# Transforms along w as 64x64 quarter products, and a second spectral layer worked in groups of 192 channels

## The chip, the core and the metric

The kernel runs on one core of one Trainium2 chip, as a single program. The metric is the device time in microseconds of one execution; the time before is the median of three runs. A profile was taken of one further execution. The engines are PE (TensorE, matrix products; its weight loads are shown apart as PEld), DVE (VectorE), ACT (ScalarE), POOL (GpSimd) and SP (SyncE, which here only issues DMAs). All data are float32, and one float32 product of the program appears in the trace as two matmul records, one for each pass.

## What is computed

The input x is one image of 48 x 48 positions with 768 channels. Four layers follow each other: an attention block with an MLP, a spectral layer (L1), a diffusion scan along channels with an output projection (L2), and a second spectral layer (L3) with weights of its own. The change concerns the two spectral layers and the places that feed them. One of them is, cut to what matters:

```python
xs = jnp.fft.rfft2(x, axes=(1, 2))              # 48 x 25 modes, 768 channels
xs = xs.reshape(B, H, Wm, NUM_HEADS, BLOCK)     # 8 blocks of 96 channels
o1r = relu(xr @ w1[0] - xi @ w1[1] + b1[0])     # per block, 96 -> 96
o1i = relu(xi @ w1[0] + xr @ w1[1] + b1[1])
o2r = o1r @ w2[0] - o1i @ w2[1] + b2[0]
o2i = o1i @ w2[0] + o1r @ w2[1] + b2[1]
out = irfft2(softshrink(o2r) + 1j * softshrink(o2i), s=(H, W))
return out + x
```

## The kernel before

Every Fourier transform is a product with a constant matrix. A spectral layer has three parts, and its data pass between them through two scratch tensors in HBM, `yu[0]` and `yu[1]`, one for each half of the channels (384 columns, `TB`).

The forward transform along w (`spectrum_rows`) takes the image in groups of eight image rows, held as four pairs of rows: 96 partitions (two rows of 48 positions) by 384 channels each. There are 12 such groups in a layer, six for each half. A group is four products with the block matrix `fw` (96 in, 112 out, L1495), four copies out of PSUM that alternate between ACT and DVE (`Evac`, L63 and L65), and one DMA to `yu` (L1497). In the first layer eleven of the groups are worked inside the MLP of the layer before, through `follow`, between the MLP's products, and the twelfth inside the spectral mix; in the second layer all twelve are worked inside the output projection of the scan (`so`, L1364), which leaves its result in SBUF as `x3`.

The mix (`spectrum_mix`) works through 40 items: 2 halves, 5 pieces of 5 frequencies (`kc`), 4 blocks of 96 channels. The items are pipelined by hand over five steps: in step n the kernel issues, in this order, the way back along h of item n-4 (`u`, L1609), the second layer of item n-3 (`z`, L1594 and L1595, then `cl` and `Z` on DVE), the first layer of item n-1 (`o`, L1573 to L1575), and the transform along h of item n (`x`, L1559). The pieces are loaded as `yt` (L1524), and the results `us` go back to `yu` (L1618), one DMA for each piece. In the first layer `yt` is added to `us` on DVE, so that the residual passes through the way back; in the second layer `us` is only copied, on ACT and DVE in turn. After each step a function `beside(step)` places other work.

The way back along w loads a group of eight rows as `gt` and multiplies it with `iw`: in the first layer by 24 products whose outputs have 96 columns (L1696), in the second by four full products (L1792), whose results DVE adds to `x3` (L1794), followed by a store to the output on ACT's queue. In the second layer the groups of half 0 go into the steps from 32 on; those of half 1 follow after the last item, with `gt` loaded in two parts, the four first pieces early and the rest after the last `us` has landed. The last group stores each pair of rows by itself.

The tile framework places semaphores by itself and may reorder instructions of one engine within its dependencies. All DMAs named here except the stores are issued by SP in the order that it is given; a DMA that waits holds those behind it.

Of the kernel before, what the change touches and what calls it, by code (L numbers as in the profile page):

```python
# [12 lines left out]
F32 = mybir.dt.float32  # L13
F32R = mybir.dt.float32r
AF = mybir.ActivationFunctionType
ALU = mybir.AluOpType
# [29 lines left out]
YR = 112  # L46
# [75 lines left out]


# [762 lines left out]
def mlp_phase(tc, ident, w1s_d, b1, w2, w2s_d, b2, ln_g, ln_b, xr_d, xa_d, follow_in):  # L886
# [8 lines left out]
    with (  # L895
# [14 lines left out]

        def psum(name):
            return pt.tile([P, 512], F32, tag="t", name=name)
# [180 lines left out]
def scan_phase(tc, ident, w, wts, rows_back, xh, x_close, c_d, cr_d, out_open):  # L1093
# [18 lines left out]
    K = 112  # L1112
# [5 lines left out]
    with tc.tile_pool(name="sc_s", bufs=1, side="left") as sp:  # L1118
# [3 lines left out]
        def out_weights():  # L1122
            wp = out_open("so_w")
            wo = wp.tile([P, 2, C], F32, tag="wo", name="wo")
            nc.sync.dma_start(wo, wo_d)
            return wo, load_bcast(nc, wp, bo_d, C, "bo", parts=BS)
# [203 lines left out]
        x3 = out_open("x3").tile([BS, NPR, C], F32, tag="x3", name="x3")  # L1330
        hg = s[ITERS % 2].rearrange("p n r t -> p (n r t)").rearrange("p (t n) -> p t n", t=NPR)
        with (
# [11 lines left out]
            def turned(j, q4):  # L1344
# [4 lines left out]
                hTs[j, q4] = tp.tile([P, 4, 2, G], F32, tag=f"hT{j}_{q4}", name=f"hT_{j}_{q4}", bufs=1)  # L1349
                nc.scalar.copy(hTs[j, q4], ps.rearrange("p (i s w) -> p i s w", i=4, s=2)[:, :, :, :G])  # L1350
# [4 lines left out]
            for half in range(2):  # L1355
                cols = slice(half * TB, (half + 1) * TB)
                for p2 in range(NPR // 2):
                    if half == 0 and p2 % 2 == 0:
                        turned(1, p2 // 2)
                    for t in range(2):  # L1360
                        pr = 2 * p2 + t
                        ps = psum(f"{pr}_{half}")
                        for j in range(2):
                            nc.tensor.matmul(ps[:BS, :TB], lhsT=hTs[j, pr // 4][:, pr % 4].rearrange("p s w -> p (s w)"), rhs=wo[:, j, cols], start=j == 0, stop=j == 1)  # L1364
                        t_ = tp.tile([BS, TB], F32, tag="t", name=f"st_{pr}_{half}")
                        V.tensor_tensor(t_, ps[:BS, :TB], bo[:, cols], ALU.add)
                        nc.scalar.activation(x3[:, pr, cols], t_, AF.Silu)
# [16 lines left out]
def block_kernel(ctx: ExitStack, tc: tile.TileContext, a: dict):  # L1384
# [69 lines left out]
    yu = [dram.tile([YR, G // 2, TB], F32, tag=f"yu{i}", name=f"yu{i}") for i in range(2)]  # L1454
    todo = []
    follow_in = lambda *args: afno_follow(nc, xa_d, a["fw2"], yu, todo, *args)
# [29 lines left out]

def spectrum_rows(nc, fw, x, yu, half, g, psum, pool, ev, name, bufs=2):

    ys = pool.tile([YR, 4, TB], F32, tag="ys", name=f"{name}_ys_{half}_{g}", bufs=bufs)
    for i in range(4):
        ps = psum(f"f_{half}_{g}_{i}")
        nc.tensor.matmul(ps[:YR, :TB], lhsT=fw, rhs=x[:, i, :], start=True, stop=True)  # L1495
        ev(ys[:, i, :], ps[:YR, :TB])
    nc.sync.dma_start(yu[half][:, 4 * g : 4 * g + 4, :], ys)  # L1497


def spectrum_open(tc, stack, name, a, layer, yu, side):  # L1500
# [3 lines left out]
    cp, yp = (stack.enter_context(tc.tile_pool(name=f"{name}_{n}", bufs=bufs, side=side)) for n, bufs in (("c", 1), ("y", 3)))  # L1504
# [16 lines left out]
    def load(half, kc):  # L1521
        if (half, kc) not in yts:
            yts[half, kc] = yp.tile([BS, KC, TB], F32, tag="yt", name=f"{name}_yt_{half}_{kc}")
            nc.sync.dma_start(yts[half, kc], yu[half][4 * KC * kc : 4 * KC * (kc + 1)].rearrange("(k q) p c -> (q p) k c", q=4))  # L1524
        return yts[half, kc]
# [4 lines left out]
def spectrum_mix(tc, name, opened, yu, psum, keep, side, halves, beside):  # L1530
# [7 lines left out]
    ev = Evac(nc)  # L1538
    HB = NB // 2
    (fh, w1t, w1s, w1d, w2t, b1t, ih), load = opened  # L1540
    with tc.tile_pool(name=f"{name}_s", bufs=2, side=side) as sp:
# [10 lines left out]
        def s_fft_h(i):  # L1552
            half, kc, b = items[i]
            if b == 0:
                ys[half, kc] = load(half, kc), sp.tile([BS, KC, TB], F32, tag="us", name=f"{name}_us_{half}_{kc}")
            yt = ys[half, kc][0]
# [9 lines left out]
        def s_mlp1(i):  # L1566
            half, kc, b = items[i]
            b += half * HB
# [18 lines left out]
        def s_mlp2(i):  # L1587
            half, kc, b = items[i]
            b += half * HB
# [13 lines left out]
        def s_ifft_h(i):  # L1603
            half, kc, b = items[i]
            Z = flow.pop(i)
            yt, us = ys[half, kc]
# [4 lines left out]
            if keep:  # L1611
                nc.vector.tensor_tensor(us[:, :, cols], pv, yt[:, :, cols], ALU.add)
# [317 lines left out]
```

## Time and profile before

| what | value |
|---|---|
| median of three runs | 3623.33 us (3620.8 to 3623.38) |
| profiled execution | 3626.7 us, span 3624.9 us, mean clock 0.987 |
| PE busy | 3539.1 us, 98% |
| DVE, ACT, POOL busy | 2002.9, 1138.5, 685.8 us |
| attention block up to its MLP | 0 to 1621 us |
| MLP, with 11 forward groups of L1 | 1621 to 2638 us |
| spectral layer L1, mix and half of its way back | 2638 to 2849 us |
| scan L2 | 2849 to 3290 us |
| output projection, with 12 forward groups of L3 | 3290 to 3386 us |
| mix of L3, with six ways back | 3386 to 3593 us |
| last reload, six ways back, stores | 3593 to 3625 us |

A row of a group of instructions gives the line, the engine, the operation, the tiles (written <- read), the shape, the count and the times; for matmuls the two numbers joined by a star are rows and columns of the array that the product uses. The record of a matmul contains its way through the array, so records of products that follow each other overlap, and the time that one takes is read from the distance between starts or from the chain of waits. The clock is the share of TensorE's full speed that was granted.

### The profile page before, as it was taken

Reading aid. Unit: us, or ns where it says so; the run is one execution under the profiler, and the core shown is the slowest. Engines: PE = TensorE matmul, PEld = TensorE weight load, DVE = VectorE, ACT = ScalarE, POOL = GpSimd, SP = SyncE. Lnnn points to the kernel's source line nnn. Section 1 sums busy time; section 2 is a strip of 40 time slices with the busy share of each in tenths; the row PEclk is TensorE's granted clock in tenths of the full one; section 3 lists DMA queues with packets and bytes.
Section 4 is the critical chain, followed back from the end, with each engine's and each line's share of the span. In section 5 each row is a group of like instructions: output and inputs, shape, how many; then the busy total and the mean of one; then the engine's idle time right before and its main releaser. Section 6 shows DMA issues by size and latency. Waiting matters only on the chain.

```text
span 3624.9 us, 52111 instructions
## 1 busy us (share of the span) xinstructions
PE 3539.1 (98%) x20914; PEld 2174.5 (60%) x20914; DVE 2002.9 (55%) x3014; ACT 1138.5 (31%) x1731; POOL 685.8 (19%) x570
## 2 busy tenths in 40 slices
PE   7999999999999999999999999999999998999998
PEld 4666654444444444555555555555578777995685
DVE  6644456767676776564244324233145478994445
ACT  1222244444555554113101210120033365223341
POOL 4211101111111110340000000000023304961131
PEclk9999999999999999999999999999999999999999
DMA  7555555656545443443345334434444303113345
GB/s 248 205 194 173 197 163 164 185 143 157 162 121 151 125 125 86 125 152 125 107 136 174 106 106 140 146 109 123 140 131 105 94 21 104 33 30 101 95 113 157
DMA packets 257371, 477.66 MB, mean 132 GB/s; under 512 B 36031, under 2 KB 209919, under 8 KB 250913
## 3 DMA queue, kind: packets, MB, share of 16 engines
q1 hardware_dynamic: 247152, 453.20, 41.8%
q10 hardware_dynamic: 9968, 21.04, 1.6%
q8 instruction: 168, 2.75, 0.3%
q14 instruction: 83, 0.67, 0.1%
HBM read 330.53 MB, written 143.62 MB: 131 GB/s over the span
## 4 chain that ended last, share of the span: by engine, by line
PE 87%; DVE 4%; DMA 3%; POOL 3%; ACT 2%; issue 1%; SPq 0%; ACTq 0%; DVEq 0%; POOLq 0%
PE p L959 14%; PE p L1022 13%; PE s L623 12%; PE av L654 12%; PE qk L361 6%; PE c L1186 4%; PE v L169 3%; PE s L633 3%; PE pj L169 2%; PE f_z L1594 2%; PE f_z L1595 2%; PE f_x L1559 2%; PE so L1364 2%; PE f_u L1609 2%; POOL t L1287 2%
## 5 line engine op out<-in xcount | busy, mean ns | idle before, releaser
L643 DVE TENSOR_TENSOR acc<-acc,p 128x928 f32<-128x928 f32 (+1 forms) x480 | 560.5, 1168 | 264.1 <-ACT p L635 222.6
L635 ACT ACTIVATE p<-s 128x928 f32<-128x928 f32 (+1 forms) x540 | 505.9, 939 | 492.2 <-PE s L633 470.2
L623 PE MATMUL s<-qt,kv 64*128 64x464 f32 (+1 forms) x2160 | 521.9, 559 | 7.8 <-DMA qt<-q_d 5.7
L1022 PE MATMUL p<-w,h 128*128 128x384 f32 x1512 | 492.7, 486 | 0.0
L654 PE MATMUL av<-p,kv 128*64 128x464 f32 (+1 forms) x2160 | 443.0, 554 | 0.0
L1022 PEld LDWEIGHTS p<-w,h 128*128 128x128 f32 x1512 | 286.2, 190 | 196.9
L633 PE MATMUL s<-bt,oneh 64*128 64x464 f32 (+1 forms) x1080 | 400.9, 731 | 0.7 <-DMA bt<-rh_d 0.7
L654 PEld LDWEIGHTS av<-p,kv 128*64 128x64 f32 x2160 | 147.0, 137 | 262.0 <-issue 250.6
L623 PEld LDWEIGHTS s<-qt,kv 64*128 64x128 f32 x2160 | 203.1, 187 | 164.8 <-issue 153.6
L959 PE MATMUL p<-x2nT,w 128*128 128x384 f32 x864 | 292.7, 488 | 2.8 <-issue 2.8
L1279 PE MATMUL c<-H,bands 128*48 128x96 f32 x5632 | 243.8, 247 | 11.2 <-issue 10.9
L361 PE MATMUL qk<-xnT,wqk 128*128 128x384 f32 x756 | 249.8, 487 | 0.3 <-DMA wqk<-wqk_d 0.3
L1279 PEld LDWEIGHTS c<-H,bands 128*48 128x48 f32 x5632 | 234.5, 123 | 20.7 <-issue 11.3
L959 PEld LDWEIGHTS p<-x2nT,w 128*128 128x128 f32 x864 | 164.8, 191 | 118.3 <-issue 4.6
L959 PE MATMUL p<-xT,w 128*128 128x384 f32 x648 | 220.7, 486 | 0.0
L998 POOL TENSOR_TENSOR rr<-rr,ml_b 128x1152 f32<-128x1152 f32 x12 | 31.8, 2648 | 954.0 <-DMA rr<-xr_d 645.5
L361 PEld LDWEIGHTS qk<-xnT,wqk 128*128 128x128 f32 x756 | 141.4, 190 | 93.3 <-issue 0.9
L954 ACT ACTIVATE h<-h,ml_b 128x384 f32<-128x384 f32 x144 | 88.3, 614 | 345.8 <-DVE h L974 173.6
L1287 POOL TENSOR_TENSOR t<-s,c 128x768 f32<-128x768 f32 x80 | 144.5, 1830 | 182.7 <-DMA bands<-in_bands_dram 171.8
L959 PEld LDWEIGHTS p<-xT,w 128*128 128x128 f32 x648 | 123.1, 190 | 85.9
L633 PEld LDWEIGHTS s<-bt,oneh 64*128 64x128 f32 x1080 | 107.0, 188 | 105.6 <-issue 103.2
L169 PE MATMUL v<-wv,xnT 128*128 128x384 f32 x378 | 133.8, 499 | 0.6 <-DVE xnT L144 0.5
(326 smaller groups left out, 4665.5 us busy)
## 6 DMA issues: line engine op xcount, KB each, us to landing
w<-w1s_d SPq DMA_DIRECT2D x36, 768.0 KB, 4.1
w<-w2s_d SPq DMA_DIRECT2D x36, 768.0 KB, 4.4
w<-w1s_d SPq DMA_DIRECT2D x36, 576.0 KB, 3.7
w<-in_mlp_w_dram SPq DMA_DIRECT2D x27, 768.0 KB, 4.6
wqk<-wqk_d SPq DMA_DIRECT2D x12, 1344.0 KB, 10.9
yu<-f_ys SPq DMA_DIRECT2D x24, 672.0 KB, 3.8
f_yt<-yu SPq DMA_DIRECT2D x20, 720.0 KB, 6.6
yu<-f_us SPq DMA_DIRECT2D x18, 720.0 KB, 4.6
```

Of the source, the lines that this page charges most:

```text
L169: nc.tensor.matmul(p[:, :TB], lhsT=rhs[n][:, c, t * P : (t + 1) * P], rhs=w[:, c, :], start=c == 0, stop=c == NC2 - 1)
L361: nc.tensor.matmul(p[:, :TB], lhsT=w[:, n, c, :], rhs=ops[sb][n][:, c, :], start=c == 0, stop=c == NC2 - 1)
L623: nc.tensor.matmul(ps[:, s, :n], lhsT=keys[pr % 2][rows, kt * P : (kt + 1) * P], rhs=held(c)[rows, :n], start=True, stop=False)
L633: nc.tensor.matmul(ps[:, s, :n], lhsT=oneh[rows, b % 2, :], rhs=bts[b // 2][rows, j, :n], start=False, stop=True)
L635: nc.scalar.activation(p, ps[:, :, :n], AF.Exp)
L643: nc.vector.tensor_tensor(probs[c], probs[c], p, ALU.add)
L654: nc.tensor.matmul(avs[c][rows, : size(c)], lhsT=vals[pr % 2][:, kt, rows], rhs=p[:, s, :], start=kt == 0, stop=kt == NT - 1)
L959: nc.tensor.matmul(p[:, :TB], lhsT=w[n][:, c, :], rhs=rhs[n][:, c, :], start=c == 0, stop=c == NC2 - 1)
L1022: nc.tensor.matmul(ps[t][:, :TB], lhsT=hs[left, f][:, t * P : (t + 1) * P], rhs=wt[:, f % KW2, :], start=f == 0, stop=f == NF2 - 1)
L1186: nc.tensor.matmul(ps[:K, i, :n], lhsT=v[:, c, tok : tok + K], rhs=w[:, cc, c0 : c0 + n], start=cc == NC - 1, stop=cc == 0)
L1279: nc.tensor.matmul(ps[r0 : r0 + G, k // 4, cols], lhsT=bands[:, n - GC, i, :] if gr else bands0[:, n, i, :], rhs=H[:, n, :, d : d + NPR], ...
L1287: GP.tensor_tensor(t, sc[:, ch], c1[:, m0 : m0 + GC].unsqueeze(2).to_broadcast([P, GC, RR, NPR]), ALU.mult)
```

## The change

The transforms along w become products of 64 x 64: 48 (or 50) rows in and 64 columns out, with the two image rows of a pair at partitions 0 and 64. A forward group is eight such products in two sets of four, one for each quarter of the array, with two PSUM tiles for a set. `yu` is laid out anew as 64 rows by 48 image rows by 384 channels, a group is written by two DMAs (one for each half of the partitions), and `x3` has 112 partitions with a gap. In the MLP the PSUM tiles of the group come from two pools in turn.

The second mix works on four groups of two blocks (192 channels), ten items each, with `yt` loaded three pieces ahead from five buffers. It adds `yt` to `us` on DVE, as the first mix does, so that the way back only copies, on ACT and DVE in turn, into `x3`. When the last piece of a group has been written, SP reloads the whole group as `gt` in two DMAs of 50 partitions, and its three ways back go into later steps (16, 18, 20 for the first group, then ten steps on). The last group is reloaded by pieces, two DMAs of 10 partitions behind each write; its last piece is written in two halves. After the last item come 12 products that nobody reads (`keep_warm`) and three ways back, each with stores on two queues. A way back is again eight quarter products, now with 2 x 192 columns.

The first layer's way back keeps its 24 products, with 128 instead of 100 rows and reloads in two DMAs.

The core of the diff:

```diff
+def keep_warm(tc, ps, left, right, n):
+    k, m = left.shape
+    for _ in range(n):
+        tc.keep_in_program_order(tc.nc.tensor.matmul(ps[:m, : right.shape[1]], lhsT=left, rhs=right, start=True, stop=True))
...
+        places = itertools.cycle(((pt, "t"), (pt, "t"), (pm, "m"), (pm, "m")))
+
         def psum(name):
-            return pt.tile([P, 512], F32, tag="t", name=name)
+            pool, tag = next(places)
+            return pool.tile([P, 512], F32, tag=tag, name=name)
...
-        x3 = out_open("x3").tile([BS, NPR, C], F32, tag="x3", name="x3")
+        x3 = out_open("x3").tile([K, NPR, C], F32, tag="x3", name="x3")
...
-                t_ = tp.tile([BS, TB], F32, tag="t", name=f"st_{pr}_{half}")
-                V.tensor_tensor(t_, ps[:BS, :TB], bo[:, cols], ALU.add)
-                nc.scalar.activation(x3[:, pr, cols], t_, AF.Silu)
+                V.tensor_tensor(x3[:, pr, cols], ps[:K, :TB], bo[:, cols], ALU.add)
+                nc.scalar.activation(x3[:, pr, cols], x3[:, pr, cols], AF.Silu)
...
-    yu = [dram.tile([YR, G // 2, TB], F32, tag=f"yu{i}", name=f"yu{i}") for i in range(2)]
+    yu = [dram.tile([HD, G, TB], F32, tag=f"yu{i}", name=f"yu{i}") for i in range(2)]
...
 def spectrum_rows(nc, fw, x, yu, half, g, psum, pool, ev, name, bufs=2):
-    ys = pool.tile([YR, 4, TB], F32, tag="ys", name=f"{name}_ys_{half}_{g}", bufs=bufs)
-    for i in range(4):
-        ps = psum(f"f_{half}_{g}_{i}")
-        nc.tensor.matmul(ps[:YR, :TB], lhsT=fw, rhs=x[:, i, :], start=True, stop=True)
-        ev(ys[:, i, :], ps[:YR, :TB])
-    nc.sync.dma_start(yu[half][:, 4 * g : 4 * g + 4, :], ys)
+    ys = pool.tile([P, 2, 2, TB], F32, tag="ys", name=f"{name}_ys_{half}_{g}", bufs=bufs)
+    for j in range(2):
+        ps = [psum(f"f_{half}_{g}_{j}_{a}") for a in range(2)]
+        for a in range(2):
+            keep = slice(a * HD, a * HD + G)
+            for b in range(2):
+                nc.tensor.matmul(ps[a][b * HD : (b + 1) * HD, :TB], lhsT=fw[keep], rhs=x[keep, 2 * j + b, :], start=True, stop=True)
+        for a in range(2):
+            ev(ys[:, j, a, :], ps[a][:, :TB])
+    for b in range(2):
+        nc.sync.dma_start(pairs_of(yu[half], b, g), ys[b * HD : (b + 1) * HD].rearrange("p j a c -> p (j a) c"))
...
         def s_fft_h(i):
-            half, kc, b = items[i]
+            group, kc, b = items[i]
             if b == 0:
-                ys[half, kc] = load(half, kc), sp.tile([BS, KC, TB], F32, tag="us", name=f"{name}_us_{half}_{kc}")
+                for ahead in range(3 if groups[group][2] < HB else 1):
+                    at = group * NKC + kc + ahead
+                    if at < len(groups) * NKC:
+                        load(*divmod(at, NKC))
+                ys[group, kc] = load(group, kc), sp.tile([BS, KC, groups[group][2] * BS], F32, tag="us", name=f"{name}_us_{group}_{kc}")
...
         def s_ifft_h(i):
...
-            if keep:
-                nc.vector.tensor_tensor(us[:, :, cols], pv, yt[:, :, cols], ALU.add)
-            else:
-                ev(us[:, :, cols], pv)
...
+            nc.vector.tensor_tensor(us[:, :, cols], pv, yt[:, :, cols], ALU.add)
+            last = kc == NKC - 1 and group == len(groups) - 1
+            if b == n - 1 or (last and b == n // 2 - 1):
+                done = slice(b // (n // 2) * (n // 2) * BS if last else 0, (b + 1) * BS)
+                put(group, kc, us, done)
...
 def load_spectrum(nc, pool, yu, half, g, name, bufs):
-    gt = pool.tile([YR, 4, TB], F32, tag="gt", name=f"{name}_gt_{half}_{g}", bufs=bufs)
-    nc.sync.dma_start(gt, yu[half][:, 4 * g : 4 * g + 4, :])
+    gt = pool.tile([P, 4, TB], F32, tag="gt", name=f"{name}_gt_{half}_{g}", bufs=bufs)
+    for b in range(2):
+        nc.sync.dma_start(gt[b * HD : (b + 1) * HD], pairs_of(yu[half], b, g))
     return gt
...
 def afno_second(tc, a, scan, yu):
...
+        GB = 2
+        groups = [(n * GB // (NB // 2), n * GB % (NB // 2), GB) for n in range(NB // GB)]
+        opened = spectrum_open(tc, stack, "f3", a, "L3", yu, "right", groups, 5)
...
-        def back(half, g):
-            cols = slice(half * TB, (half + 1) * TB)
-            gt = gts.pop((half, g))
-            last = half == 1 and g == NTB - 1
-            for i in range(4):
-                ps = psum(f"w_{half}_{g}_{i}")
-                nc.tensor.matmul(ps[:BS, :TB], lhsT=iw, rhs=gt[: 4 * KW, i, :], start=True, stop=True)
-                dst = x3[:, 4 * g + i, cols]
-                nc.vector.tensor_tensor(dst, ps[:BS, :TB], dst, ALU.add)
...
+        def put(group, kc, us, cols):
+            half, b0, _ = groups[group]
+            cs = slice(b0 * BS + cols.start, b0 * BS + cols.stop)
+            nc.sync.dma_start(spectrum_of(yu[half], kc, cs), us[:, :, cols])
+            if kc == 0:
+                gts[group] = bp.tile([P, G // 2, W], F32, tag="gt", name=f"f3_gt_{group}")
+            if group == final or kc == NKC - 1:
+                rows = slice(2 * KC * kc if group == final else 0, 2 * KC * (kc + 1))
+                for b in range(2):
+                    nc.sync.dma_start(gts[group][b * HD + rows.start : b * HD + rows.stop, :, cols], yu[half][rows, b * (G // 2) : (b + 1) * (G // 2), cs])
+
+        def store(queue, prs, cols):
+            for s in range(2):
+                queue.dma_start(out[s, :, prs, cols], x3[s * HD : s * HD + G, prs, cols])
+
+        def back(group, c):
+            cols = channels(group)
+            gt = gts[group].rearrange("p (j s) c -> p s j c", s=2)
+            for j in range(2):
+                ps = [psum(f"w_{group}_{c}_{j}_{b}") for b in range(2)]
+                for b in range(2):
+                    keep = slice(b * HD, b * HD + KR)
+                    for s in range(2):
+                        nc.tensor.matmul(ps[b][s * HD : (s + 1) * HD, : 2 * W], lhsT=iw[keep], rhs=gt[keep, s, 4 * c + 2 * j : 4 * c + 2 * j + 2, :], start=True, stop=True)
+                for b in range(2):
+                    ev(x3p[:, b, 4 * c + 2 * j : 4 * c + 2 * j + 2, cols], ps[b][: HD + G, : 2 * W].rearrange("p (j c) -> p j c", j=2))
+                if group == len(groups) - 1:
+                    store((nc.scalar, nc.sync)[j], slice(8 * c + 4 * j, 8 * c + 4 * j + 4), cols)
+            if group < len(groups) - 1:
+                store(nc.scalar, slice(8 * c, 8 * c + 8), cols)
+
+        each = NKC * GB
+        backs = {each * (q + 1) + 6 + 2 * c: (q, c) for q in range(final) for c in range(3)}
...
+        spectrum_mix(tc, "f3", opened, psum, "left", groups, put, beside)
+        keep_warm(tc, psum("warm"), opened[0][0], opened[0][1][:, :2].rearrange("p n r c -> p (n r c)"), 12)
+        for c in range(3):
+            back(final, c)
```

## The prediction

> **What bounds the kernel now.** I read the engine table first, then the windows by stage, then the timeline and the chain of waits of the places that the change touches. The sums are made against the profiled execution: 3626.7 us, span 3624.9, which is 3.4 above the median of the runs shown (3623.33); a change measured on the one is taken off the other.
>
> ```profile
> PE 3539.1 (98%) x20914; PEld 2174.5 (60%) x20914; DVE 2002.9 (55%) x3014; ACT 1138.5 (31%) x1731; POOL 685.8 (19%) x570
> ```
>
> TensorE is busy for 98% of the span, so a product taken off it counts where it has no slack. The windows (stretch, length, busy time of PE, PEld, DVE, ACT, POOL, clock, DMA share, GB/s): MLP, output projection of layer 2, second spectral mix, end.
>
> ```profile
> 1621.00:2637.80 1016.80, 1015.65 (x3184) 596.49 (x3185) 335.02 (x662) 148.60 (x255) 30.66 (x13) 1.00 0.41 130
> 3290.00:3386.00 96.00, 94.97 (x308) 49.01 (x306) 40.85 (x74) 38.82 (x79) 3.01 (x2) 1.00 0.35 104
> 3386.00:3593.00 207.00, 203.21 (x1568) 165.36 (x1568) 106.30 (x209) 76.67 (x180) 58.56 (x80) 0.98 0.39 108
> 3593.00:3624.90 31.90, 18.98 (x48) 9.05 (x48) 13.29 (x24) 0.00 (x0) 0.00 (x0) 0.78 0.71 206
> ```
>
> In the first three the next busiest engine, DVE, is at 33, 43 and 51%, PE at 98 to 100. The last is different: the chain of waits shows what it is made of.
>
> ```profile
> 3382.39 2.58 PE so_f L1495 x8
> 3384.97 1.15 issue
> ...
> 3592.96 4.98 DMA yu<-f_us
> 3597.99 2.77 DMA f_gt<-yu
> 3600.90 18.99 PE f_w L1792 x48
> ```
>
> Two rows give the unit. One forward group (L1495) is four full products of 384 columns, eight records, 2.58 us: 0.645 us a product. At the end 24 such products take 18.99 us where 24 x 0.645 is 15.5: the other 3.5 us are the clock: finer windows show it granted at 0.50 from 3600 to 3605, after PE sat idle for 8.7 us.
>
> Does TensorE overlap small products? The timeline of attention:
>
> ```profile
> 699.76 4.89 PE L654 MATMUL av<-p,kv 128*64 128x464 f32 x24
> ...
> 705.68 0.94 PE L623 MATMUL s<-qt,kv 64*128 64x464 f32 x4
> 706.09 0.73 PE L633 MATMUL s<-bt,oneh 64*128 64x464 f32 x2
> 706.66 0.94 PE L623 MATMUL s<-qt,kv 64*128 64x464 f32 x4
> ```
>
> A record of 464 columns alone would take 0.3225 x 464/384 = 0.39 us. 24 records on column halves (128*64) take 4.82 in the chain, 0.20 each; a period of four records plus two on row halves (64*128) takes 0.98. So halves run two at a time, column halves with two moving streams through each row, row halves with two PSUM banks written at once. No row shows both at once, four 64x64 quarters.
>
> **The forward transform** (24 groups). Four full products become eight quarter products, two sets of four. If the four quarters of a set overlap, a set lasts 0.645 and a group 1.29. Changing shape costs too: record by record, the first score product starts 482 ns after the last of L654 instead of 389, and the first of L654 662 after L633 where the next score starts after 565: 95 ns a change, 0.19 a group. So 1.48 instead of 2.58: 1.10 saved. Bounds: four at a time 1.48; two at a time, all that the rows show, 8 x 0.645/2 + 0.19 = 2.77. I take four at a time, because each resource that it needs (two streams in a row, two banks in a partition) is shown working by one of the two halves.
>
> - 11 groups in the MLP: 12.1 saved. There the fourth product stood behind a full one (f_f x6, p x2, f_f x2 in the timeline); if the two sets are split like that, another 0.19 each. I take 10.0 (bounds 8 to 12).
> - One group at the start of the first mix, where PE waits for the filling pipeline anyway: 0.5 (0 to 1.1).
> - 11 groups between the projection's products, where PE has no gap: 12.1. The twelfth is followed by the first product of the mix 3.9 us after its start (2.58 and the 1.15 "issue", in which the last copies free PSUM); with copies on two engines in sets about 2.6: 1.3. Together 13.4. What remains per group (5.16 + 1.48) is above DVE's 4 x 0.55 + 2 x 0.56 and ACT's 4 x 0.52 + 2 x 0.48.
>
> The projection's 112 instead of 96 output rows cost nothing on PE: L1495 with 112 and L1364 with 96 both take 2.58 for four. The copy of hT grows from 0.48 to some 0.55 on an ACT that is 40% busy.
>
> **DMAs.** Forward writes and the first layer's reloads are split in two: 24 more issues of 0.30 to 0.43 on SP, and 14% more bytes. SP has slack except behind the last write of the first mix, where the reload (5.75 us) ends a wait of 1.68 us of PE: +1.0 (0 to 2).
>
> **The second mix.** 40 items of 4.57 us stay. Adding yt on DVE for all instead of copying on ACT and DVE in turn costs nothing: the first mix already does that and its u products also stand 4.57 apart (2654.78, 2659.35). Up to item step 40 there were 3 ways back of 2.58; now 8 of 1.48: 11.8 - 7.7 = +4.1 (two at a time: +14.4). Their four copies are shared by ACT and DVE (0.48, 0.56) and the stores, now on ACT's queue ahead of the next step's copies, take 2 x 0.32; ACT is 37% busy here.
>
> **The added wait.** After each of the first three groups SP issues the last write of us and then, behind its landing, the whole group's reload; the next group's yt loads queue behind that. The way back is due 16.4 us after that us (4 steps less what went before). The write landed in 2.7 (c_d, 336 KB) to 4.98 us; the reload is 2400 packets of 768 bytes, 36 to 41 ns each in the records, 5.4 to 6.2 us on 16 engines; the nearest landings are 10.2 (wsc, 1839 KB) and 8.8 (oT, 2304 KB). Together 12 to 16: hidden, barely. yt is fetched two pieces before its use, and the one behind the reload lands some 6 us early. I take +2 in all (0 to +20, if each reload lands 6 us late).
>
> The Trainium skill speaks against this reload: by "DMA: Bandwidth & Descriptors", section "Why a DMA increments its semaphore by 16 and not by 1", a load of 50 partitions runs on 10 engines, not 16. By that it takes 8.6 to 9.9 us of packets and some 3.5 more per group, and PE would wait 0 to 4 us three times: an estimate of +6 where I have +2. No DMA of such a shape is in this trace.
>
> **The end**, from u of step 40 (3574.75 before; 50.15 us to the end of the span). Now, in us from that product: u 0.81, z 1.70, o 1.21, way back 1.48, u, z: 7.7. Before, ways back stood between z and the next u; now PE waits for cl and Z (0.2 + 2 x 0.65 + 0.1): u of item 38 at 9.3, z of 39 to 11.8, wait, u of 39 at 13.4, us ready at 15.0 (before 18.2). SP: first half-piece of us written at 11.1, landed 15.1 (4.0 between the 2.7 and 4.98 above), two reloads issued (0.43 each), and only then the second write, 16.0: landed 20.0, reloads issued and landed (2.77 in the chain) 23.2. Before, this point was 26.0. The 12 unread products (7.7 us of PE) fill 14.2 to 21.9, so they are covered by this wait, and the clock stays up; were the reload there at once, they would cost those 7.7. Then three ways back: PE 3.9, but ACT sets the pace with two copies, two issues and a wait, 1.7 each, so the last copy is at 24.2 + 5.1 = 29.3, the last stores are issued at 30.0 and land in 3.7 (L1796 before): 33.7 instead of 50.15: -16.4 (bounds 30 to 37: -20 to -13).
>
> Sum: -10.0 - 0.5 - 13.4 + 1.0 + 4.1 + 2.0 - 16.4 = -33.2: 3623.3 - 33.2 = 3590 (profiled 3593.5).
>
> **Rivals.**
> 1. Quarters overlap two at a time, like the halves. The mechanism sits in L1495 and L1792: a product's two records follow each other on one quarter, and nothing shows the engine reaching past three quarters' waiting records. Forward 23 x (+0.19) = +4.4, mix +14.4, waits and DMAs +3; at the end one group in step 40 costs +1.29 and the last three +3.9, less the ACT pace that they hide: 37.4, -12.7. Sum +9.1: 3632, slower. Some 34 groups are on the path, so the gain is gone when a group takes 1.48 + 33.2/34 = 2.46 us; from there on it is slower. For it: only pairs are seen. Against: nothing in the rows is used up by pairs.
> 2. The reloads miss their time: 4 to 6 us of PE three times, 12 to 18: 3600 to 3608.
> 3. The gain is partial: sets overlap by less than four (a group near 2.0, 34 x 0.5 = 17), or the end keeps its length because 0.38 us issues, four landings in a row and 1.8 MB of stores set it: 3605 to 3618.
>
> The skill has a row on the first: "TensorE: Matmul & The Clock Gate", "Measured speedup vs the span model", gives 10.6 for 16 tiles. That share of the ideal would let a set of four do the work of 2.65 at a time and make a group 2.1 us, an estimate by which the sum shrinks to about -11. Its loss comes from single bursts; the pairs here reach 0.20 of 0.39, no loss, and I follow the trace.
>
> **Numbers.** Forecast 0.66; rival 2, 0.12; rival 3, 0.08; rival 1, 0.14. The bounds of the forecast's terms give 3581 to 3598 (longer waits are rival 2); 2 us below are for durations from one execution, and the range reaches over rivals 2 and 3 to 3618. 0.2% (7 us) is about what a measurement can tell: faster (under 3616) 0.66 + 0.12 + 0.06, less a little for bounds, 0.80; same 0.06; slower 0.14.
>
> **What would show it.** Right: groups of L1495 about 1.4 us in the chain of waits; the mix at 4.57 us an item with ways back of 1.5; clock 1.00 in the end; the last products 4 us; some 20 us from the last us to the end instead of 32. Wrong: quarter records that start in pairs; PE idle before the first way back of a group, ended by the DMA of gt; DVE or ACT before the products of the projection.

## The result, and the profile after

The changed kernel takes 3614.67 us (median; 3610.95 to 3618.72), beside 3620.16 of the kernel before on the same chip: ratio 0.9985, 95% interval 0.9979 to 0.9992. It is 5.5 us faster where I had forecast 33. The profiled execution took 3612.97 us, span 3611.2. Of its 13.7 us against the span before, 6.0 arise ahead of the MLP (its first product stands at 1615.34 instead of 1621.32) in code that the change does not touch; that is scatter between executions. From the MLP on it is 7.8. The engine table, then the windows of the four stages (stretch, length, busy time of PE, PEld, DVE, ACT, POOL, clock, DMA share, GB/s):

```profile
PE 3517.6 (97%) x21226; PEld 2155.7 (60%) x21226; DVE 2002.4 (55%) x3010; ACT 1142.4 (32%) x1735; POOL 685.6 (19%) x570
```

```profile
1615.00:2621.30 1006.30, 1004.29 (x3272) 587.22 (x3272) 334.12 (x663) 148.57 (x255) 30.41 (x12) 1.00 0.44 132
3273.00:3359.00 86.00, 84.58 (x406) 40.16 (x404) 41.46 (x75) 39.62 (x80) 3.15 (x2) 1.00 0.50 124
3359.00:3587.00 228.00, 215.68 (x1667) 171.05 (x1668) 116.22 (x222) 76.06 (x178) 58.95 (x80) 0.93 0.48 113
3587.00:3611.10 24.10, 13.24 (x70) 6.85 (x68) 3.35 (x6) 2.58 (x6) 0.00 (x0) 0.85 0.60 112
```

MLP and projection are as full as before and shorter. The mix has become longer: PE stands idle in it for 12 us, and its clock fell from 0.98 to 0.93. Term by term, in us, from the starts of the same products in both traces:

| term of the forecast | forecast | measured |
|---|---|---|
| MLP, first to last product | -10.0 | -11.4 (1015.16 to 1003.81) |
| first layer and scan | +0.5 | 0.0 (649.12 to 649.17) |
| projection, to the first product of the mix | -13.4 | -9.4 (100.52 to 91.07) |
| mix, to the u of step 40 (ways back, waits) | +6.1 | +21.7 (188.63 to 210.38) |
| the end, from there | -16.4 | -8.8 (50.15 to 41.40) |

The quarters do what they should. In the chain of waits in the projection a group takes 1.45 us where it took 2.58:

```profile
3280.90 1.45 PE so_f L1516 x16
3282.35 2.76 PE so L1375 x8
```

The mix is lost where the ways back of a group begin. The chain there goes through the last write of `us`, then the reload:

```profile
3420.01 3.19 DMA yu<-f_us
...
3423.62 15.89 DMA f_gt<-yu
...
3439.65 2.40 PE f_w L1854 x12
```

The timeline of PE has the wait, the list of waits its sum, and two windows show what runs meanwhile and afterwards:

```profile
3439.65 2.40 PE L1854 MATMUL f_w<-f_gt,iw 50*64 50x384 f32 x12 [2.08 <-DMA f_gt<-yu]
```

```profile
PE f_w L1854 <- DMA f_gt<-yu: 8.6, 4, 2.9
```

```profile
3438.00:3440.00 2.00, 0.35 (x5) 0.24 (x9) 0.00 (x0) 0.17 (x1) 0.90 (x2) 1.00 0.68 208
3440.00:3447.00 7.00, 7.00 (x35) 4.45 (x28) 1.77 (x3) 0.48 (x1) 0.00 (x0) 0.51 0.49 118
```

A reload takes 15 to 17 us from issue to landing, PE waits 2.1 us, and then runs for 7 us at half clock. From u to u a step with a way back lasts 6.12 us and the next 4.65; at the three boundaries it is 9.95 and 7.00, 10.35 and 7.43, 7.97 and 4.65: 15.0 us too much. The rest of the 21.7 is 5.2 for the ways back, where the forecast had 4.1, and 1.5 at the start of the mix: 17.79 us from its first product to its first u instead of 16.31, with 13.7 us at half clock instead of 10.2. That start lasts between 15.56 and 18.27 us in the runs of this case. At the end SP issued the reload of piece 3 and both of piece 4 behind the last write, six DMAs at once:

```profile
3586.89 3.17 DMA yu<-f_us
...
3590.13 7.80 DMA f_gt<-yu
3597.93 0.24 issue
3598.17 1.43 PE f_w L1854 x10
```

### The profile page after: what moved, and what is told of

Read it like the earlier page. It is cut to its first block, busy times and chain, and to the rows that moved or that the text cites. A ratio compares the mean times of both kernels' runs of the same rounds, so it can differ in the third digit from the quotient of the medians.

```text
span 3611.2 us, 52825 instructions
## 1 busy us (share of the span) xinstructions
PE 3517.6 (97%) x21226; PEld 2155.7 (60%) x21226; DVE 2002.4 (55%) x3010; ACT 1142.4 (32%) x1735; POOL 685.6 (19%) x570
## 4 chain that ended last, share of the span: by engine, by line
PE 86%; DVE 6%; DMA 4%; ACT 2%; issue 1%; POOL 1%; SPq 0%; ACTq 0%; DVEq 0%; POOLq 0%
PE p L970 14%; PE p L1033 13%; PE s L631 12%; PE av L662 12%; PE qk L369 6%; PE c L1197 4%; PE v L177 3%; PE s L641 3%; PE pj L177 2%; PE so L1375 2%; DVE s L1310 2%; PE f_u L1648 2%; PE f_z L1633 2%; PE f_z L1632 2%; DVE H L1294 2%; PE f_x L1597 2%
## 5 line engine op out<-in xcount | busy, mean ns | idle before, releaser
L1632 PE MATMUL f_z<-f_w,f_o 97*96 97x96 f32 x800 | 137.7, 255 | 0.0
```

What stands on the lines that cost most here:

```text
L1632: nc.tensor.matmul(out, lhsT=o1[:, j, 1:3, :].rearrange("c r h -> c (r h)"), rhs=w2t[:, b, 0, :], start=True, stop=False)
```

## The experiments

Each starts from the changed kernel. Its ratio is that to runs of the kernel before on the same chip, the changed kernel's own being 0.9985. "Mix" is the time from the first to the last u (188.81 before, 207.97 after), "end" that from the last u to the end of the span (33.67 and 26.02). The theories were A (the reload runs on too few DMA engines), B (its packets are small and slow), C (the ways back themselves disturb the mix), later D (its two DMAs slow each other) and E (its addresses collide).

**Where the 15 us of the mix went**

*e1, sixteen engines.*

```diff
-rows = slice(2 * KC * kc if group == final else 0, 2 * KC * (kc + 1))
+rows = slice(2 * KC * kc, 2 * KC * (kc + 1)) if group == final else slice(0, HD)
```

> The reload of each of the first three groups takes all 64 rows of the scratch tensor (the last 14 are zeros) instead of 50: 3072 packets of 768 bytes instead of 2400. Theory A (too few DMA engines: 50 partitions are spread over ten): the two DMAs now run on sixteen, 3072 x 40 ns / 16 = 7.7 us of packets, so the reload lands 10 to 11 us after its issue instead of 16, although it moves 28% more. PE's waits for gt at the three boundaries go, with them the half clock behind them; the boundary steps last 6.1 and 4.6 us, the mix is 13 to 15 us shorter, the whole 3600 to 3602. Theory B (the packets are slow, 60 to 85 ns each, on however many engines, because they are scattered 768-byte reads beside writes of us and loads of yt): landing 16 to 20 us after issue, PE's waits as long or 2 to 4 us longer, the whole 3614 to 3626.

Ratio 0.9972 (0.9961 to 0.9983), mix 202.94. The windows of the changed kernel's first reload and of this one:

```profile
3424.00:3438.00 14.00, 13.57 (x115) 11.13 (x113) 7.76 (x15) 5.33 (x14) 4.68 (x7) 1.00 0.77 151
```

```profile
3427.00:3441.00 14.00, 13.67 (x116) 11.24 (x114) 7.87 (x15) 5.32 (x14) 4.68 (x7) 1.00 1.03 178
```

and in its chain of waits:

```profile
3427.14 14.87 DMA f_gt<-yu
```

The engines were there (a share over 1 is packets that overlap), yet the reload, with 28% more bytes, landed 14.4 to 14.9 us after its issue instead of 14.8 to 17.0, 1.2 us earlier in the mean. A holds in part. Other transfers are not what slows the packets: in these two windows, the changed kernel's and then this one's, no other DMA of the mix is in flight.

```profile
3427.00:3429.00 2.00, 2.00 (x19) 1.52 (x18) 1.13 (x3) 1.32 (x3) 0.71 (x1) 1.00 0.72 133
```

```profile
3430.00:3432.00 2.00, 2.00 (x19) 1.52 (x18) 1.13 (x4) 1.32 (x3) 0.60 (x1) 1.00 1.15 184
```

In the packet records the first 400 to 550 packets of a reload take 36 ns each; then they take 60 to 70 on ten engines (some 165 a microsecond) and 75 on sixteen (240).

*e2, ways back of the first two groups two steps later.*

```diff
-backs = {each * (q + 1) + 6 + 2 * c: (q, c) for q in range(final) for c in range(3)}
+backs = {each * (q + 1) + (8 if q < 2 else 6) + 2 * c: (q, c) for q in range(final) for c in range(3)}
```

> The ways back of the first two groups are placed two steps later (18, 20, 22 and 28, 30, 32), so that each reload has 25 us instead of 16 until its use; the DMAs themselves are unchanged. The third group stays where it was. Theories A and B both say that the reload lands in time whatever makes it slow: the two boundary waits go, and with them the half clock, 6.3 + 7.1 = 13.4 us of the u-to-u distances; the third boundary keeps its 1.9 us; the whole 3600 to 3602. Theory C (the mix lost its 15 us not to these waits but to the ways back themselves, whose eight quarter products and copies between the mix's stages disturb the pipeline, the stretched steps only being where it shows): the stretched steps move with the ways back to steps 18 and 28 and stay as long, the whole stays within 3 us of 3615.

Ratio 0.9966 (0.9952 to 0.9979), mix 201.28. At the first two boundaries every step is 6.12 or 4.65: C falls. But the third became 13.31 and 7.41. The stores of the second group's last way back now ran beside the third group's last write, which landed after 6.43 us instead of 3.23:

```profile
3524.53 6.43 DMA yu<-f_us
3531.35 15.62 DMA f_gt<-yu
```

*e8, contiguous scratch tensor: four tensors, one for each group.*

```diff
+yu = [dram.tile([HD, G, TB // 2], F32, tag=f"yv{i}", name=f"yv{i}") for i in range(4)]
...
-yu[half][rows, b * (G // 2) : (b + 1) * (G // 2), cs]
+yu[group][rows, b * (G // 2) : (b + 1) * (G // 2), cols]
...
```

> The scratch tensor of the second layer is split into four, one for each group of 192 channels, so that the reload of a group reads 18 KB without a break for each partition and half instead of 24 pieces of 768 bytes; bytes, partitions (50, so the same engines) and issue order stay. The forward writes become four DMAs for a group of rows, with pieces of 768 bytes. Theory B (the reload is slow because of its many small packets, 60 to 75 ns each once two such DMAs are in flight): larger packets, the reload lands 8 to 11 us after its issue instead of 14.8 to 17, the boundary steps of the mix fall to 6.1 and 4.6, the mix is 13 to 15 us shorter, the whole 3600 to 3603. Theory A (ten engines are what limits it): 1.84 MB on ten engines at the 160 GB/s of the changed kernel stay at 14 us or more, the boundary steps stay within 1 us, the whole 3612 to 3616. The forward writes may cost the projection 0 to 2 us.

Ratio 0.9954 (0.9940 to 0.9968), mix 200.27. Packets are now 18,432 bytes and most take 1.2 to 1.3 us each, so an engine moves 15 GB/s; landings after 14.5 to 15.4 us, so that B, which asked for 8 to 11, falls as the whole cause. With landings only 1.0 us earlier in the mean, the boundary steps lose 8.9 us instead of 15.0. *e14* adds the 64 rows of e1:

> The scratch tensor by groups of e8 (18 KB without a break) together with the 64 rows of e1 (sixteen engines). Theory A with B (each engine moves 15 GB/s of large packets as in e8, and sixteen of them 240): 2.36 MB in 9.8 us, landing 11 to 12 us after issue, boundary steps 6.1 and 4.6, the whole 3600 to 3602. Rival (all engines together move no more than the 185 GB/s that e1 and e13 held): landing 13.5 to 14.5 us, boundary steps as in e8 or 1 us better, the whole 3604 to 3608.

Ratio 0.9957 (0.9944 to 0.9971), mix 200.95, landings 13.4 to 14.7: the rival's landing, though at more than its 185 GB/s. The windows of the first reload, e8 and then e14:

```profile
3423.00:3435.00 12.00, 12.00 (x104) 10.31 (x102) 7.08 (x14) 3.87 (x10) 3.49 (x5) 1.00 0.73 164
```

```profile
3424.00:3435.00 11.00, 11.00 (x98) 9.48 (x97) 6.06 (x12) 3.42 (x9) 4.11 (x6) 1.00 1.01 215
```

*e12 and e13, another spacing of the rows* (400 elements instead of 384; e13 with 64 rows too).

> The second layer gets a scratch tensor of its own whose rows of 384 channels are spaced by 400 elements instead of 384, so that two neighbouring partitions of the reload read 76,800 bytes apart instead of 73,728. Packets (768 bytes), partitions (50) and issue order stay as in the changed kernel. Theory E (the reload is slow because the ten engines read at the same time at a stride that is a multiple of 8 KB, and so in the same part of the memory; loads of yt, whose neighbouring partitions are 1.5 KB apart, have packets of 36 ns): packets of the reload fall from 60 to 75 ns to about 40, 2400 x 40 / 10 = 9.6 us, the reload lands about 11 us after its issue instead of 15 to 17, the boundary steps fall to 6.1 and 4.6, the mix is 13 to 15 us shorter, the whole 3600 to 3603. Rival (two such DMAs in flight slow each other on the ten engines whatever they read): landing and boundary steps as in the changed kernel, the whole 3612 to 3617.

> The same spacing, and 64 rows in the reload (zeros included) instead of 50, so that it runs on sixteen engines. With the changed kernel, e1 and the run before this makes a square of engines by spacing. Theory E with A: 3072 x 40 / 16 = 7.7 us of packets, landing 9 to 10 us after issue, boundary steps of 6.1 and 4.6, the whole 3600 to 3602, no faster than ten engines with the spacing, since both are in time. Rival (neither spacing nor engines, the packets stay at 66 to 76 ns): landing 14 to 15 us as in e1, the mix 5 to 8 us shorter than in the changed kernel, the whole 3609 to 3612.

Ratios 0.9985 (0.9976 to 0.9994) and 0.9971 (0.9959 to 0.9983), as without the spacing; landings 15.6 to 15.9 and 14.4 to 15.1. E falls.

*e18, the two halves of the reload one after the other.*

```diff
...
+nc.sync.dma_start(gts[group][:HD], yu[half][:, : G // 2, cs])
+nc.sync.dma_start(gts[group][HD - 1 : P - 1], raw[half][:HD, G // 2 :, cs])
...
```

> As e1 (64 rows, sixteen engines), but the second half of a group's reload is issued only after the first half has landed (its destination begins one partition earlier and so overlaps that of the first). It shows what makes packets of 36 ns take 60 to 76. Theory D (the two halves in flight at once slow each other): packets of each half about 36 to 45 ns, DMA near 300 GB/s or more while a half is alone, each half lands 4 to 6 us after its issue. Rival (the packets of such a reload are slow by themselves once a queue is filled): each half moves at 180 GB/s, 8 us from issue to landing. The time of the whole is not the question here.

One run, 3626.83 us. A half alone lands after 9.0 and 9.4 us, nearer the rival's 8 than the 4 to 6 of D, and moves 185 GB/s (3428.3 to 3430.6). The first half of e1, with the second in flight, had landed after 9.0 us too. D falls:

```profile
3424.86 9.02 DMA f_gt<-yv
3433.90 9.41 DMA f_gt<-yv
```

*e16, forty rows of the reload one piece earlier.*

```diff
-if group == final or kc == NKC - 1:
-    rows = slice(2 * KC * kc if group == final else 0, 2 * KC * (kc + 1))
+if group == final or kc >= NKC - 2:
+    rows = slice(0 if group != final and kc == NKC - 2 else 2 * KC * kc, 2 * KC * (kc + 1))
```

> The first three groups are no longer reloaded whole behind their last write: rows 0 to 39 go out behind piece 3, one piece (9 us) earlier, and only rows 40 to 49 behind piece 4; bytes, packets and engines as in the changed kernel. If the boundary waits and the clock behind them are the 15 us that the mix lost (theories A and B alike), the boundary steps fall to 6.1 and 4.6, the mix from the first to the last u lasts 193 us instead of 208, the whole 3600 to 3602. Rival (the waits come from transfers that are in each other's way, whenever they are issued: stores, writes and loads of yt land later in turn, as the third boundary of e2 showed): a new wait for yt or for gt of 2 to 5 us at each boundary, the mix at 200 us or more.

Ratio 0.9984 (0.9975 to 0.9993), mix 209.84: the rival. The first boundary got better (7.38 and 4.65), the others worse (10.92 and 7.12, 12.74 and 7.99), because the early reload now stood ahead of the last write on the same engines, and that write landed after 13 us:

```profile
3472.02 12.96 DMA yu<-f_us
3485.00 5.15 DMA f_gt<-yu
```

*e20, all ways back one step later, nothing else.*

```diff
-backs = {each * (q + 1) + 6 + 2 * c: (q, c) for q in range(final) for c in range(3)}
+backs = {each * (q + 1) + 7 + 2 * c: (q, c) for q in range(final) for c in range(3)}
```

> The changed kernel with the ways back of all three groups one step later (17, 19, 21 and so on), the DMAs unchanged. A reload of 15 to 16 us behind a write of 3.2 then stands against 21 us instead of 16.4. Theory A or B, whichever makes it slow: the boundary steps fall to 6.1 and 4.6, the mix is 13 to 15 us shorter, the third group's last way back stands beside the last items, where PE waits anyway; the whole 3600 to 3603. Rival (as in e2: the stores of the later ways back keep the next group's last write and reload from starting in time): one or two boundaries are clean, another costs 7 to 10 us, the whole 3608 to 3612.

3597.09 us (3595.89 to 3600.15), ratio 0.9939 (0.9926 to 0.9953). The mix takes 190.12; there is no wait for `gt` before the last u. In its chain of waits the first boundary now reads:

```profile
3436.51 0.81 PE f_u L1648 x2
3441.08 1.45 PE f_w L1854 x16
3442.53 0.98 PE f_u L1648 x2
```

The reload is as slow as ever and costs nothing. To the u of step 40 the mix takes 194.86, 15.5 less than in the changed kernel. That is +6.2 against before, where the forecast had +6.1; the two agree by chance, as is shown below at the ways back.

**The projection**

*e3, full products in the second layer's forward transform.*

```diff
...
+for b in range(2):
+    nc.tensor.matmul(ps[b][:, :TB], lhsT=fw.rearrange("p a k -> p (a k)"), rhs=x[:, 2 * j + b, :], start=True, stop=True)
...
```

> The forward transform of the second spectral layer alone is made with full products again (112 rows in, 128 columns out, block matrix), everything else as in the changed kernel; its writes go out in four DMAs for a group. It prices the quarter products in the projection. Theory A (the quarters are what shortened the projection, less than I forecast because each change of shape between the projection's products and the quarters costs PE 0.17 us): a group lasts 2.58 instead of 1.45 us in the chain, the eight products of the projection 5.16 instead of 5.34, the periods are 8.3 and 7.75 as in the kernel before, the projection 9 to 11 us longer, the whole 3624. Rival (the projection gained from the bias added in place, SiLU in place, or the copies grouped in sets): the projection only 1 to 4 us longer, the whole 3616 to 3619.

Ratio 1.0013 (1.0004 to 1.0022); the projection takes 100.68 us again (100.52 before), so the quarters are all of its gain. Its chain:

```profile
3287.46 2.60 PE so_f L1515 x8
3290.06 5.16 PE so L1375 x16
```

*e11, two forward groups after each other.*

```diff
-if n and n % 2 == 0:
+if n and n % 4 == 0:
+    rows_in(n // 2 - 2, scan_psum)
     rows_in(n // 2 - 1, scan_psum)
...
```

> In the projection of layer 2 two forward groups follow each other every four steps instead of one every two, so that PE changes between the full products and the quarters half as often. Theory A (a change of shape between 128x112 and 64x64 products costs PE 0.17 us, 0.35 for a group): five such pairs fewer, the projection 1.7 to 2 us shorter. Rival (copies out of PSUM: eight tiles are wanted where six are there, and the second group waits for DVE and ACT): the projection as long or up to 5 us longer.

Ratio 0.9980 (0.9970 to 0.9989), projection 89.54. A period with two groups takes 14.48 and then 13.24 us instead of twice 7.41 and twice 6.80, 0.34 and 0.36 less for one change to quarters and back. Two groups take:

```profile
3285.61 2.74 PE so_f L1516 x32
```

**The end**

*e5, writes and reloads of the last group in the order of the text*, by `keep_in_program_order` on each.

> The issue order of the last group's writes and reloads on SP is held to the order of the text: the reload of piece 3 before the writes of piece 4, and the reload of piece 4's first half before the write of its second half. In the changed kernel the reloads of piece 3 and of both halves went out together behind the last write, at 3587.3 to 3590.5. Theory A (six reloads on ten engines at once make the last one slow: 7.8 us from issue to landing): the last reload finds the engines free, lands some 4 us after issue, the first way back starts 3.5 to 4 us earlier, the whole is 3.5 to 4 us shorter, 3611. Rival (what ends last is the chain of the last write and its own reload, or stores that are bound by bytes): the last landing comes at most 1 us earlier, or SP, which now waits for landings between the writes, sends the last write 1 to 2 us later: the whole within 2 us of 3615.

Ratio 0.9986 (0.9977 to 0.9995), end 26.73. SP waited for each landing, so the last write went out 6.4 us after the last u instead of 1.7; but the last reload, alone on its engines, landed in 3.2:

```profile
3593.44 3.86 DMA yu<-f_us
3597.32 3.20 DMA f_gt<-yu
```

*e9, another order: first write of piece 4, reload of piece 3, reload of piece 4's first half, second write and its reload.*

> Only the order on SP at the end is changed, otherwise than in the pinned run before: write of the first half of piece 4, then the reload of piece 3, the reload of piece 4's first half, then the write of the second half and its reload. SP is then never kept from a write that is ready. Theory A (six reloads in flight at once make the last 7.8 us long): piece 3 is reloaded at about 3582.7 instead of 3587.3 on the time of the changed kernel, the last reload lands 3.2 to 4 us after its issue as in the pinned run, the first way back starts 3.5 to 4 us earlier, span 3607 to 3608 when the stages before are as long. Rival (the end is bound by the stores, 1.77 MB at the 173 GB/s that its last window shows): the first way back is earlier but the last store lands less than 1 us earlier.

Ratio 0.9975 (0.9963 to 0.9986), end 23.06, 3.0 less. In its chain nothing is left between the unread products and the first way back:

```profile
3584.98 9.43 PE f_warm L130 x24
3594.42 1.33 PE f_w L1860 x10
```

*e4, without the unread products* (the `keep_warm` call left out).

> The 12 unread products before the last ways back are left out. If they do what I costed (cover the wait of PE at no cost and keep the clock up): the last three ways back run at half clock for 3 to 7 us, PE's part of them 5.5 to 7 us instead of 4.1, the end 0.5 to 2 us longer, since ACT and the stores set its pace. Rival (they stand in the way): the first way back starts earlier and the end is 0.5 to 2 us shorter. Both are within the scatter of the whole time, so the profile decides.

Ratio 0.9983 (0.9974 to 0.9993); the last products run at half clock (6.05 us in the chain for 40 records), and the end is 27.84, 1.8 longer. Of this, 1.2 arise ahead of the first way back, in a u at half clock (1.90 us instead of 1.03) and a reload of 8.46 us instead of 7.80; what comes behind its start is 0.6 longer, and no more than that can be put down to the products.

**Sums**

*e17, e16 with e9 and e11.*

> The reload by pieces, the order of e9 at the end and the paired forward groups of e11 together. If the terms add up: 15 us of the mix, 3 us of the end, 1.5 us of the projection against the changed kernel: 3614.7 - 19.5 = 3595, span near 3592. If the reload by pieces brings new waits: 3602 to 3607.

Ratio 0.9972 (0.9962 to 0.9981), mix 212.61: e16's waits again.

*e19, e14 with the ways back one step later, e9 and e11.*

> e14 (contiguous scratch tensor by groups, 64 rows), the ways back one step later, the order of e9 at the end and the paired forward groups of e11. If the terms add up: 14 us of the mix, 3 us of the end, 1.5 to 2.5 us of the projection against the changed kernel: about 3595, span 3592 to 3594. If a store collides with a write at one boundary: 3600 to 3604.

Ratio 0.9940 (0.9926 to 0.9953), no better than e20 alone; end 27.50.

*e21, e20 with the third group's ways back in steps 37, 38, 39.* In e20's end the last write waits for a store of that group, whose semaphore it uses:

```profile
3564.11 10.13 DMA out_dram<-x
...
3574.31 3.20 DMA yu<-f_us
```

> e20, with the third group's ways back in three steps one after the other (37, 38, 39) instead of 37, 39, 41. In e20 the last two writes of us were issued only at 3572.04 and 3574.31, when the stores of that group's last way back, issued at 3563.75 and 3564.11, had landed: SP waits there for the semaphores that those stores use. Theory (this wait is what made e20's end 28.2 us from the last u instead of 26.0): with the stores 5 to 9 us earlier the last write goes out 1.7 us after the last u as in the changed kernel, the end is 24 to 26 us, the whole 3593 to 3595. Rival (the place of the last way back filled a wait of PE for Z, which now comes back): the last three items take 2 to 3 us longer and the whole stays at 3595 to 3598.

Ratio 0.9935 (0.9922 to 0.9949). Both were right: the end fell from 28.22 to 24.11, and the last items took 4.0 us longer (mix 194.07). *e22, with e9 and e11 as well:*

> e21 with the order of e9 at the end and the paired forward groups of e11. If the terms add up: 3 us less at the end and 1.5 us less in the projection than e21, 3589 to 3592. If the end is already free of SP's waits in e21, or the stores set it: 3592 to 3595.

Ratio 0.9943 (0.9930 to 0.9957), end 27.38: the last write, issued while other reloads ran, landed after 6.6 us. The terms do not add up here; e19 to e22 cannot be told apart, and the simplest of them is e20.

## Why the prediction was right or wrong

- **Quarters four at a time: right.** 16 records in 1.45 us against the 1.48 forecast; rival 1 falls with it, and the MLP gained 11.4. The Trainium skill's table ("TensorE: Matmul & The Clock Gate", "Measured speedup vs the span model") had let me estimate 2.1; these runs show no such loss, and the measurement decides.
- **The step that failed: "The added wait", +2 in all.** The reload was costed at 36 to 41 ns a packet on sixteen engines, 5.4 to 6.2 us, from the records of short DMAs (480 packets), and its landing by the 8.8 and 10.2 us of loads into 128 partitions with packets of 3072 and 2452 bytes. A long reload with packets of 768 bytes holds 36 ns only at its start. Measured, it ran on ten engines at some 60 ns: 2400 x 60 / 10 = 14.4. Write and reload took 18 to 20 us, not 12 to 16, against the 16.4 that I had rightly named as due. The term was 15.0 instead of 2. The lists of waits give 6 of it; the half clock behind the first two waits lasts 6.8 us each time and so costs nearly 7 in all, which I had priced at the end but not here; 2 are not assigned. e20 shows the step alone: with the place moved and the reload as slow, the boundary steps are 6.12 and 4.65 and the 15 us are gone.
- **Ways back in the mix, 1.1 over.** Each costs 1.63 (6.12 + 4.65 - 2 x 4.57) and not 1.48; the change of shape is the 0.35 of e11 instead of 0.19. That e20 meets the +6.1 of the forecast is luck: its wait is nothing where the forecast had 2, and these 1.1 and a start of the mix that took 1.1 longer than before (17.40) fill the place.
- **Rival 2** (4 to 6 us of PE three times) is what happened, with less waiting and more clock. I had put it at 3600 to 3608; what rival 3 says of the end came on top.
- **The skill's rule on engines** ("DMA: Bandwidth & Descriptors", "Why a DMA increments its semaphore by 16 and not by 1") agrees with the trace: with only a reload in flight the DMA share is 0.72 in the changed kernel and 1.15 with the 64 rows of e1, as 10 to 16. My estimate by it, +6, was nearer than my own +2, but the engines were not the larger part: e1 has sixteen and lands 1.2 us earlier.
- **Projection, 4.0 short.** The change of shape was sized at 0.19 a group from attention; here the periods shrink by 0.88 and 0.94, not 1.10 (2.1 in eleven groups), and e11 prices the change at 0.35. The twelfth group gained nothing: 3.93 us from its start to the mix, as before (3.89), where I took 1.3. The remaining 0.6 is the start of the stage, which differs by as much between executions.
- **The end, 7.6 short.** On the scale of the forecast: `us` ready at 17.1 (15.0), because z and u ran at half clock after the wait for Z; last write landed at 20.3 (20.0); reload landed at 28.2 (23.2), as I had not seen six reloads in flight at once; from there to the end 13.2 (10.5), with stores at 173 GB/s. e9 shows 3.0 of the 5.0; the stores' part was not tried alone. That the unread products cost nothing is right, since PE waits another 2.57 us behind them, and so is that they keep the clock: 1.00 from 3598 to 3604, where e4 has 0.52 from 3602 to 3608.
- **The range** held the time, since it reached over rivals 2 and 3; the chance of 0.66 for the forecast alone was too high for a sum in which one transfer was "hidden, barely".

## What to carry to other kernels

Cost a long transfer by one that is like it in length, packets and partitions: packet times of short DMAs are those of a start, and the long loads that the prediction went by had larger packets and more partitions. Where a wait ends on the path, add what the clock takes afterwards, and place the consumer with a margin of a whole step: one number changed in the schedule (e20) was worth three times as much as the whole change. Before moving a transfer, look at which write, store or semaphore stands behind it on the same queue and engines; in e2, e5, e16, e20 and e22 a wait came back there.

## What the runs showed of the hardware

- Reload packets of 768 bytes start at 36 ns and settle at 60 to 75 after some 400 to 550 packets. With only a reload in flight, ten engines moved 133 GB/s and sixteen 184; with packets of 18 KB, windows that hold other transfers too show 164 and 215. Engines and packet size explain a part of it; spacing, the other half and other transfers explain nothing that shows. What the limit is stays open. Not tried was the number of partitions that one DMA of a reload fills, 50 or 64 in all these runs. In the kernel before, five reloads of 112 partitions in a row, with packets of 6144 bytes on sixteen engines, moved 287 GB/s, more than e14 with packets three times as large:

```profile
3499.00:3509.00 10.00, 10.00 (x86) 8.33 (x85) 5.00 (x10) 4.42 (x11) 3.52 (x5) 1.00 1.01 287
```

- A wait of 2.1 us was followed by 7 us at half the granted clock (0.51 from 3440 to 3447). The length of the wait alone does not decide it: behind 1.04 us in e14 the clock was 0.53 (3439 to 3446), behind 2.21 us in e9 0.76 (3440 to 3447), and in e1 a wait of 1.47 us cost no clock and one of 1.37 us did (8.43 and 4.65 at the first boundary, 8.61 and 7.62 at the second).
- Four 64 x 64 quarters of float32 run fully beside each other: 16 records take 1.45 us and 32 take 2.74 (e11), so that the second 16 take 1.29, a quarter of 16 x 0.3225. A change between full products and quarters, there and back, costs 0.35 us.
